# A twelve-layer decoder kernel: the first rounds of its state-space layer written out by hand, and that layer's end interleaved with the start of the 8-head attention layer

## The chip, the cores and the metric

The kernel runs on one core of one Trainium2 chip. The time is that of one launch on the device, in microseconds (us); of several runs the median is taken. The engines of the core, as the profile names them, are PE (TensorE, matrix products; PEld is its weight load), DVE (VectorE), ACT (ScalarE), POOL (GpSimd) and SP (SyncE, which here only issues DMAs). Each engine works through its own list of instructions in order and waits for the others through semaphores.

## The reference

The input x is 32 sequences of 128 tokens with 128 features, in float32. Twelve layers follow, each of the form x = x + f(layernorm(x)). Only the first two are touched by the change:

```python
x = x + _L0_attn_ref(_layernorm(x), ...)              # state-space layer
x = x + _L0_xattn_ref(_layernorm(x), ctx_1024, ...)   # 8-head attention
```

The state-space layer projects each token to a gate z, to 512 channels and to 32 step sizes dt. It runs a causal convolution of four taps over the channels and applies silu. The channels are then x (256), B (128) and C (128). The recurrence over tokens is computed in chunks: products C·B weighted by exponentials of running sums of dt·A, times dt·x, and a carried state. The result y gets a skip term, is gated and normalized, goes through an output projection and a layer norm and is added:

```python
y = Y + D_skip * x;  y = y * silu(z)
y = y * rsqrt(mean(y * y) + 1e-5) * norm_w
out = y @ out_proj_w.T
ln = (out - mean) * rsqrt(var + 1e-5) * ln_w + ln_b
return x + ln            # x here is the normalized input of the layer
```

The 8-head layer takes queries from x, and keys and values from both x and a context of the same shape (256 keys in all), with heads of 64:

```python
q1, k1, v1 = x1 @ Wq1, x1 @ Wk1, x1 @ Wv1;  k2, v2 = x2 @ Wk2, x2 @ Wv2
attn = softmax(q1 @ concat(k1, k2).T * 64**-0.5)
out = (attn @ concat(v1, v2)) @ Wo + bo
```

The tenth layer's feed-forward half multiplies by an int8 weight, `wq`, which the change also touches.

## The kernel before, in words

The 32 sequences are held as 8 groups (G) of 4 (J). A group is a tile `xg[i]` of 128 partitions (tokens) by 4 x 128. The layers run one after another over all groups. Within a layer the work is a list of rounds, one per sequence, numbered n = 4·i + j (group i, sequence j). A helper `go` (line 893) advances a generator by one step, so that a step of a later group can stand in a round of an earlier one. `follow(T, A, V)` (line 901) makes PE, ACT and DVE keep the order in which the program issues their instructions, until `follow()` (line 950). POOL and SP, and whatever is issued outside such a stretch, are placed by the framework's scheduler. Nearly every instruction is recorded under line 194, a helper, so that the profile is read by tile names.

**The state-space layer, `layer0` (line 662).** Its steps are these.

- `entry(g)` (742): mean and variance on DVE, a power on POOL (732), four ACT instructions that write the normalized `xn`, an addition on POOL, four PE transposes and an ACT copy to `xnT`.
- `decays(g)` (751): the step sizes and their exponentials (tiles `dts`, `dA`).
- `conv(g, c)` (689), for each of four channel blocks c: one PE product of 128x512 and an ACT copy to a `bmid` tile; an ACT scaling into a `gmid` tile; three DVE multiply-adds; an ACT tanh; a last DVE multiply-add. Each of these is a step.
- `gate(g, b)` (709): the same for z.
- `first(n)` (781), `second(n)` (810), `exponentials(n)` (821), `weighted(n, h)` (826), `third(n)` (831): the chunked products of one sequence, spread over three rounds. POOL builds their operands (lines 799, 804, 806).
- `joined(g)` (853): closes a group. DVE combines the sums (tile `bmid`), ACT squares them, PE does the output projection and the sums of squares (`ps<-w,bmid` and, with a single output column, `ps<-cs,bmid`), then come the norms on DVE, POOL and ACT and three POOL instructions that update `xg[g]`.

The loop at line 902 runs n from -9 to 33. Rounds -9 to -3 do only entry, decays and conv steps, one at a time, since `first(0)` comes in round -2. Rounds 32 and 33 only close the last group.

**The 8-head layer, `layer1` (954).** `prepare(i, 0)` loads a group of the context by DMA and normalizes x (BN statistics on DVE, then lines 394 to 397 on POOL). `prepare(i, 1)` transposes both. `project_in(n)` (967) makes queries and keys, `project_values(n)` (981) values, `scores(n, c2)` (989) half of the scores, with exponentials (1004) and scaling (1011). Ahead of its loop the layer does all of this for the first sequences in one straight run, and only then begins its rounds: transposes of the probabilities (1018), the weighted sum (1030), the output projection (1042), and the scores of the next sequence.

**Buffers.** Tiles come from pools with a fixed number of buffers under one name: PSUM `ps`, `two` and `acc` two each; `gbig` 3, `bbig` 4, `gmid` 10, `bmid` 5, `xn` and `xnT` 2 each. A tile waits until the buffer that it takes over is no longer read. During the state-space layer all three `gbig` and one `bbig` are held throughout (its `kept` and `more`), and the weights `w0` occupy one of the four `units` buffers.

**Loads.** SP issues, in this order: the constants `cs` (line 278), the eight groups of x (284), weight units 0 to 2 (304), the 16 KB of `wq` (1654), and the first context group (323). ACT issues `w0`, `ww` and two more weight loads. The cast of `wq` to bf16 stands in `layer9`, outside any kept order.

Of the kernel before, what the change touches and what calls it, by code (L numbers as in the profile page):

```python
# [25 lines left out]
G = 8  # L26
J = 4
# [177 lines left out]
def program(ctx, tc, cols, x, ctxt, mask, drop, dfirst, dsmall, dwide, drows, dunits, dexperts, dconst, drel, dwq, out):  # L205
# [23 lines left out]
    def gbig(shape=(128, 2048), dtype=F32):  # L229
        return big.tile(list(shape), dtype, tag="gbig", name="gbig", bufs=3)  # L230
# [7 lines left out]
    def bmid(shape=(128, 512)):  # L238
        return mid.tile(list(shape), F32, tag="bmid", name="bmid", bufs=5)
# [5 lines left out]
    def follow(*engines):  # L245

        for e in (V, A, T):
            e.keep(e in engines)
# [26 lines left out]


    cs = const.tile([128, cconst.n], F32, name="cs")
    SY.dma_start(out=cs, in_=dconst)
    K = {n: cconst.view(cs, n) for n in cconst.at}
    ident = K["ident"]  # L280
    xg = []
    for i in range(G):
        t = const.tile([128, J, D], F32, name=f"x{i}")
        SY.dma_start(out=t, in_=x[i * J : i * J + J].rearrange("b s d -> s b d"))
        xg.append(t)
        if i == 0:
            w0 = units.tile([128, cfirst.n], F32, tag="unit", name="w0")
            A.dma_start(out=w0, in_=dfirst)
            ww = const.tile([128, cwide.n], F32, name="ww")
            A.dma_start(out=ww, in_=dwide.to_broadcast([128, cwide.n]))  # L290
            wr = const.tile([1, crows.n], F32, name="wr")
            A.dma_start(out=wr, in_=drows)
# [24 lines left out]
    flip = const.tile([128, 128], BF16, name="flip")  # L317
    V.tensor_copy(flip, W0["flip"])
    ctxT = [const.tile([128, 512], F32, name=f"ctxT{i}") for i in range(G)]

    def load_ctx(i):
        t = gmid((128, J, D))
# [336 lines left out]

    def layer0():
        na = const.tile([128, 32], F32, name="na")
        A.activation(na, WW["m_A_log"], AF.Exp)
        V.tensor_scalar(na, na, -1.0, None, ALU.mult)
# [187 lines left out]
        def joined(g):  # L853

            ys, sq = [], []
            for b in range(2):
                y = bmid((128, J, 128))
                for ch in (1, 0):
                    at = slice(64 * ch, 64 * ch + 64)
                    V.scalar_tensor_tensor(y[:, :, at], convs[g, b][:, :, at], W0["D"][:, b : b + 1], sums[g][ch][:, b], ALU.mult, ALU.add)  # L860
                ys.append(y)
            for b, y in enumerate(ys):
                V.tensor_tensor(y[:, :, 64:128], y[:, :, 64:128], offs[g][:, b], ALU.add)
                V.tensor_tensor(y, y, zs.pop((g, b)), ALU.mult)
            yield
            for y in ys:
                q = bmid((128, J, 128))
                A.activation(q, y, AF.Square)
                sq.append(q)
            yield  # L870
            op, msp = ps((128, J, 128)), ps((128, J))
            for j in range(J):
                for b in range(2):
                    mm(op[:, j], ys[b][:, j], W0["out"][:, b * 128 : b * 128 + 128], b == 0, b == 1)
            for j in range(J):
                for b in range(2):
                    mm(msp[:, j : j + 1], sq[b][:, j], K["ones"][:, 0:1], b == 0, b == 1)
            ln = bmid((128, J, 128))
            A.copy(ln, op)
            yield  # L880

            rs, r2 = small(J), small(J)
            V.tensor_scalar(rs, msp, 1.0 / 256, 1e-5, ALU.mult, ALU.add)
            V.reciprocal(r2, rs)
            P.tensor_tensor(rs, rs, K["nhalf"], ALU.pow)
            for _ in normalize(ln, ln, rs, r2):
                yield
            P.tensor_tensor(ln, ln, bc(WW["m_ln_w"], 1, J), ALU.mult)
            P.tensor_tensor(xg[g], xg[g], bc(WW["m_ln_b"], 1, J), ALU.add)
            P.tensor_tensor(xg[g], xg[g], ln, ALU.add)  # L890
            yield

        def go(what, g, *more):

            if 0 <= g < G:
                key = what, g, *more
                if key not in late:
                    late[key] = what(g, *more)
                next(late[key], None)

        follow(T, A, V)
        for n in range(-9, G * J + 2):
            i, j = n // J, n % J

            g, c = (i + 1, j) if j < 2 else (i + 2, j)
            go(conv, g, c)
            if 0 <= n + 2 < G * J:
                first(n + 2)
            go(conv, g, c)
            if j == 0:  # L910
                go(joined, i - 1)
                go(gate, i, 0)
            elif j == 1:
                go(joined, i - 1)
            elif j == 2:
                go(decays, i + 2)
                go(decays, i + 2)
            elif j == 3:
                go(decays, i + 2)
                go(gate, i + 1, 1)  # L920
                go(entry, i + 3)
            if 0 <= n + 1 < G * J:
                second(n + 1)
            go(conv, g, c)
            if 0 <= n + 1 < G * J:
                exponentials(n + 1)
                weighted(n + 1, 0)
            if 0 <= n < G * J:
                third(n)
            if 0 <= n + 1 < G * J:  # L930
                weighted(n + 1, 1)
            go(conv, g, c)
            if j == 0:
                go(joined, i - 1)
                go(joined, i - 1)
            elif j == 1:
                go(joined, i - 1)
                go(joined, i - 1)
                go(joined, i - 1)
                go(entry, i + 2)  # L940
            elif j == 2:
                go(decays, i + 2)
                go(decays, i + 2)
                go(gate, i + 1, 1)
            elif j == 3:
                go(entry, i + 3)
                go(entry, i + 3)
                go(gate, i + 1, 0)
            go(conv, g, c)
        follow()  # L950

    def layer1(then):
        ua, ub = U[0], U[1]
        ctxs, normal, sources, keys, queries, values, probs, outs, heads = ({} for _ in range(9))

# [9 lines left out]
        def project_in(n):  # L967
            i, j = n // J, n % J
            at = slice(j * 128, (j + 1) * 128)
            if n % 2 == 0:  # L970
                keys[n // 2] = gbig((128, 2, 4, 256))
            q, k = gmid((128, 4, 128)), keys[n // 2][:, n % 2]
            for w, src, o, copy in ((0, sources[i], q, A.copy), (1, sources[i], k[:, :, 0:128], V.tensor_copy),
                                    (2, ctxT[i], k[:, :, 128:256], A.copy)):
                p = ps((128, 4, 128))
                for c in range(4):
                    mm(p[:, c], ua[:, w * 512 + c * 128 : w * 512 + c * 128 + 128], src[:, at])
                copy(o, p)
            queries[n] = q
# [70 lines left out]
                add_x(i, outs.pop(i))  # L1050

        last = G * J
        follow(T, A, V)
        prepare(0, 0)
        prepare(0, 1)
        project_in(0)
        for c2 in range(2):
            for step in scores(0, c2):
                step()
        prepare(1, 0)  # L1060
        project_in(1)
        project_values(0)
        for n in range(last + 1):
            i, j = n // J, n % J
            ahead = n + 1 < last
            if n < last:
                if ahead:
                    e0 = scores(n + 1, 0)
                transposes(n, 0)
                if ahead:  # L1070
                    e0[0]()
            if n > 0:
                project_out(n - 1)
            if n < last:
                transposes(n, 1)
                if ahead:
                    e0[1]()
                    e1 = scores(n + 1, 1)
                if j == 1 and i + 1 < G:
                    prepare(i + 1, 1)  # L1080
                if n + 2 < last:
                    project_in(n + 2)
                if ahead:
                    e1[0]()
                    project_values(n + 1)
                    e1[1]()
                weighted(n)
                if j == 0 and 0 < i and i + 1 < G:
                    prepare(i + 1, 0)
                if i == G - 1:  # L1090
                    next(then)
        follow()


    def layer2():
# [554 lines left out]


    def layer9():
        wq8 = const.tile([128, 32], I32, name="wq8")
        SY.dma_start(out=wq8, in_=dwq)
        V.tensor_copy(wq, wq8.bitcast(I8))
        p = ps()
        mm(p[:, 0:32], W["a3_Wk"], W["a3_kp"])
        kf = const.tile([128, 32], F32, name="kf")
# [158 lines left out]
        return first, second, third, lambda: project(i, st["yT"], W["x3_W"], WW["L3_xattn_bout"])  # L1817


    wq = const.tile([128, 128], BF16, name="wq")  # L1820

    def layer11(i):

        rnd = 1.5 * 2.0**23
# [38 lines left out]
        return first, second, third, last  # L1863

    load_units(0, 1, 2, 3, 4)
    layer0()
    load_units(5)
    lead2, run2 = layer2()
    layer1(lead2)
    load_units(6, 7)  # L1870
    lead3, run3 = attention16(layer3(), layer4())
    run2(lead3)
# [41 lines left out]
```

## Time and profile before

| | us |
|---|---|
| median of 3 runs | 3098.97 |
| lowest and highest run | 3094.29, 3100.82 |
| the profiled execution | 3108.52 |
| its span, first to last instruction | 3106.7 |

So 1.8 us of the profiled execution lie outside its span, and it took 9.5 us longer than the median. The mean granted TensorE clock over the span was 0.903.

In the span, PE was busy for 2576.8 us (83%), DVE for 2106.3 (68%), ACT for 1509.0 (49%) and POOL for 996.4 (32%). The state-space layer takes roughly the first 450 us of the span and the 8-head layer runs from there to about 870 us.

A line of the chain of waits gives start, duration and what the chain went through at that time. A line of the timeline gives start, duration, engine, line, operation, output <- input with the shape, the count and, in brackets, how long the engine had been idle and what released it. A line of the stage table gives a stretch of the span, its length, each engine's busy time in it with the number of instructions, the granted TensorE clock (1.00 is full speed), the mean share of the DMA engines and GB/s.

### The profile page before, as it was taken

The page shows a single profiled execution, that of the slowest core. Times are in us where ns is not written, and L with a number is a line of the kernel's source. Part 1 is how long each engine was busy: PE and PEld are TensorE (multiplying, and loading weights), DVE is VectorE, ACT ScalarE, POOL GpSimd, SP SyncE. Part 2 cuts the span into 40 slices and gives each one's busy share as a digit, 9 for nine tenths or more (in the row PEclk, how much of TensorE's full clock was granted, in tenths as well). Part 3 has the DMA queues.
Part 4 walks back from the last instruction along what each step waited for, and adds up shares of the span by engine and source line. Part 5 has one row for each costly group of instructions (what it writes and reads, how often), then busy time and mean ns, then how long its engine had stood idle before and what let it go on. Part 6 is the DMA issues. An engine that isn't in the chain of part 4 may idle for free.

```text
span 3106.7 us, 55574 instructions
## 1 busy us (share of the span) xinstructions
PE 2576.8 (83%) x22554; PEld 1651.8 (53%) x22554; DVE 2106.3 (68%) x4228; ACT 1509.0 (49%) x3411; POOL 996.4 (32%) x1034
## 2 busy tenths in 40 slices
PE   4887889999989988888887999978886869886554
PEld 2555556777744445556664444445553657543433
DVE  4776747888788756667877555458895328777883
ACT  3555534444422245556654445447772226555563
POOL 3343332322210122234542000034434355424444
PEclk8888879999989999999999999979997889997777
DMA  3000000000000000000000000000003243100000
GB/s 108 2 2 2 5 19 4 8 8 1 11 11 1 0 31 2 5 8 9 8 5 15 1 1 1 0 1 2 1 2 125 79 150 106 62 18 14 21 11 21
DMA packets 50146, 68.35 MB, mean 22 GB/s; under 512 B 3681, under 2 KB 41570, under 8 KB 49762
## 3 DMA queue, kind: packets, MB, share of 16 engines
q1 hardware_dynamic: 42608, 33.84, 3.5%
q0 software_dynamic: 6848, 27.81, 2.7%
q8 instruction: 178, 2.92, 0.4%
q10 hardware_dynamic: 434, 3.14, 0.3%
q14 instruction: 78, 0.64, 0.1%
HBM read 51.11 MB, written 13.68 MB: 21 GB/s over the span
## 4 chain that ended last, share of the span: by engine, by line
PE 51%; DVE 30%; ACT 7%; POOL 7%; issue 3%; DMA 1%; another core or an unknown queue 1%; SPq 0%; POOLq 0%; DVEq 0%; ACTq 0%
PE ps L194 22%; PE two L194 15%; PE acc L194 14%; DVE bbig L194 12%; DVE s L194 9%; DVE bmid L194 4%; DVE gmid L194 3%; ACT bbig L194 3%; POOL xn L397 3%; POOL gbig L477 2%; ACT bmid L194 2%; POOL s L395 1%; ACT gmid L194 1%; ACT gbig L194 1%; DVE x L194 1%
## 5 line engine op out<-in xcount | busy, mean ns | idle before, releaser
L194 PE MATMUL ps<-cs,bbig 128*128 128x128 f32 x2208 | 330.9, 290 | 77.8 <-ACT bbig L194 43.4
L194 ACT COPY bbig<-ps 128x512 f32<-128x512 f32 x416 | 226.9, 586 | 270.3 <-PE ps L194 270.0
L194 PEld LDWEIGHTS ps<-cs,bbig 128*128 128x128 f32 x2208 | 255.9, 147 | 183.7 <-ACT bbig L194 98.0
L194 DVE TENSOR_REDUCE s<-two 128x8 f32<-128x1024 f32 (+1 forms) x192 | 234.2, 1220 | 143.5 <-PE two L194 142.4
L194 PE MATMUL two<-xnT,u 128*128 128x512 f32 x512 | 264.5, 617 | 14.0 <-DVE bmid L194 7.8
L194 DVE TENSOR_TENSOR bbig<-bbig 128x256 f32<-128x256 f32 (+4 forms) x394 | 274.3, 749 | 2.0 <-ACT bbig L194 1.0
L194 PE MATMUL acc<-bmid,u 128*128 128x512 f32 x448 | 238.5, 619 | 29.6 <-DVE bmid L194 28.2
L194 PE MATMUL two<-gbig,gmid 32*128 32x512 f32 (+1 forms) x1280 | 205.9, 578 | 32.9 <-POOL gbig L477 32.0
L477 POOL TENSOR_SCALAR gbig<-bmid,cs 128x512 f32<-128x512 f32 x96 | 148.6, 1564 | 209.0 <-ACT bmid L194 209.0
L194 DVE TENSOR_TENSOR bmid<-bmid,ps 128x512 f32<-128x512 f32 x192 | 129.9, 684 | 109.1 <-ACT bmid L194 90.3
L194 ACT ACTIVATE bbig<-bbig 128x1024 f32<-128x1024 f32 (+1 forms) x160 | 141.8, 887 | 94.7 <-DVE bbig L194 94.2
L194 ACT ACTIVATE bbig<-two,s 128x256 f32<-128x256 f32 (+1 forms) x384 | 153.9, 439 | 26.9 <-DVE s L194 23.5
L194 ACT ACTIVATE bmid<-two 128x512 f32<-128x512 f32 x104 | 61.7, 596 | 196.3 <-PE two L194 186.4
L194 PEld LDWEIGHTS two<-xnT,u 128*128 128x128 f32 x512 | 92.6, 194 | 119.1 <-issue 55.2
L194 PEld LDWEIGHTS acc<-bmid,u 128*128 128x128 f32 x448 | 80.7, 195 | 130.2 <-DVE bmid L194 72.6
L194 DVE TENSOR_TENSOR bbig<-two,s 128x1024 f32<-128x1024 f32 (+1 forms) x128 | 139.7, 1092 | 8.6
L194 ACT ACTIVATE bmid<-two,ws 128x512 f32<-128x512 f32 x128 | 85.2, 686 | 117.7 <-PE two L194 115.8
L1014 POOL TENSOR_TENSOR bbig<-bbig,s 128x1024 f32<-128x1024 f32 x32 | 60.6, 1893 | 238.6 <-PE two L194 154.4
L194 ACT ACTIVATE bbig<-bbig,s 128x128 f32<-128x128 f32 x384 | 118.8, 388 | 24.2 <-DVE s L194 24.2
L194 PE MATMUL ps<-cs,xn 128*128 128x128 f32 x288 | 66.2, 318 | 72.8 <-ACT xn L194 31.4
L489 POOL MEMSET val<- 128x512 f32 x72 | 39.0, 543 | 260.8 <-PE acc L194 260.0
L194 PEld LDWEIGHTS two<-gbig,gmid 32*128 32x128 f32 (+1 forms) x1280 | 82.0, 191 | 73.9 <-POOL gbig L477 35.2
(291 smaller groups left out, 5976.9 us busy)
## 6 DMA issues: line engine op xcount, KB each, us to landing
u<-in_units SPq DMA_DIRECT2D x10, 768.0 KB
gmid<-in_ctx SPq DMA_DIRECT2D x16, 256.0 KB, 2.6
xs<-bbig SPq DMA_DIRECT2D x4, 903.0 KB, 6.0
xt<-xs SPq DMA_DIRECT2D x28, 129.0 KB, 3.0
x<-in_x SPq DMA_DIRECT2D x8, 256.0 KB, 10.6
gmid<-in_mask SPq DMA_DIRECT2D x8, 256.0 KB, 3.3
ys<-bbig SPq DMA_DIRECT2D x2, 1024.0 KB
gmid<-ys SPq DMA_DIRECT2D x8, 256.0 KB, 5.3
```

Of the source, the lines that this page charges most:

```text
L194: d = f(*args, **kwargs)
L395: P.tensor_tensor(rs, rs, K["nhalf"], ALU.pow)
L397: P.tensor_scalar(xn[:, j, :], xg[i][:, j, :], mv[:, j, 0:1], rs[:, j : j + 1], ALU.subtract, ALU.mult)
L477: P.tensor_scalar(o[:, n, :], k, K["n4"][:, n : n + 1], None, ALU.mult)
L489: P.memset(o, 0.0)
L1014: (V if c2 else P).tensor_tensor(pr[:, four, :], pr[:, four, :], bc(nm[:, four], 2, 256), ALU.mult)
```

## The change

Four things are done.

1. **Loads at the start.** The DMA of `xg[0]` is issued before that of the constants `cs`. The load of `wq` keeps its place on SP's queue, and its cast, which stood in `layer9`, is issued in round 3 of the 8-head layer, inside the kept order.
2. **First rounds of the state-space layer.** Rounds -9 to -3 of the loop are replaced by a list of 33 steps written out by hand. It contains the same steps: `entry(0)`, `entry(1)`, `decays(0)` and the four convolutions of group 0, but with the convolutions overlapping one another. The loop starts at -2.
3. **The start of the 8-head layer moves into the last rounds of the state-space layer.** `layer1` returns a generator `lead`. Its parts are issued at the ends of rounds 27 to 31 (load and normalize group 0; transposes; `project_in(0)`; `project_in(1)`; load and normalize group 1) and, after the loop, between the steps of `joined(7)`: the scores of sequence 0, then their exponentials, the values and the scaling. The keys of the first two sequences go to a `bbig` buffer, since the three `gbig` are still held.
4. **The closing of the last group moves into the first rounds of the 8-head layer.** `joined(7)` uses `gmid` instead of `bmid` tiles. Its last norm, three steps, is returned to `run1`, which advances it by one step at the end of rounds 0 and 1 and finishes it in round 2.

The diff, cut to its core:

```diff
     cs = const.tile([128, cconst.n], F32, name="cs")
-    SY.dma_start(out=cs, in_=dconst)
...
         if i == 0:
+            SY.dma_start(out=cs, in_=dconst)
...
-    def layer0():
+    def layer0(lead):
...
             ys, sq = [], []
+            tile_of = gmid if g == G - 1 else bmid
...
-            yield
+            if g < G - 1:
+                yield
...
-        for n in range(-9, G * J + 2):
+
+        go(entry, 0)
+        go(entry, 0)
+        go(entry, 0)
+        go(entry, 1)
+        go(entry, 0)
+        go(decays, 0)
+        go(conv, 0, 2)
+        go(entry, 1)
+        go(decays, 0)
+        go(conv, 0, 2)
+        go(conv, 0, 3)
+        go(conv, 0, 2)
+        go(conv, 0, 3)
+        go(entry, 1)
+        go(conv, 0, 2)
+        go(conv, 0, 3)
+        go(conv, 0, 0)
+        go(conv, 0, 2)
+        go(conv, 0, 0)
+        go(decays, 0)
+        go(conv, 0, 3)
+        go(conv, 0, 0)
+        go(entry, 1)
+        go(conv, 0, 3)
+        go(decays, 0)
+        go(conv, 0, 1)
+        go(conv, 0, 1)
+        go(conv, 0, 0)
+        go(conv, 0, 1)
+        go(decays, 0)
+        go(conv, 0, 0)
+        go(conv, 0, 1)
+        go(conv, 0, 1)
+        for n in range(-2, G * J):
...
             go(conv, g, c)
+            if n >= G * J - 5:
+                next(lead)
+        go(joined, G - 1)
+        next(lead)
+        go(joined, G - 1)
+        next(lead)
+        go(joined, G - 1)
         follow()
+        return late[joined, G - 1]
...
-                keys[n // 2] = gbig((128, 2, 4, 256))
+                keys[n // 2] = (gbig if n else bbig)((128, 2, 4, 256))
...
-        follow(T, A, V)
-        prepare(0, 0)
-        prepare(0, 1)
-        project_in(0)
-        for c2 in range(2):
-            for step in scores(0, c2):
-                step()
-        prepare(1, 0)
-        project_in(1)
-        project_values(0)
-        for n in range(last + 1):
+
+        def lead():
+            prepare(0, 0)
+            yield
+            prepare(0, 1)
+            yield
+            project_in(0)
+            yield
+            project_in(1)
+            yield
+            prepare(1, 0)
+            yield
+            steps = [step for c2 in range(2) for step in scores(0, c2)]
+            yield
+            steps[0]()
+            steps[2]()
+            project_values(0)
+            steps[1]()
+            steps[3]()
+            yield
+
+        def run(others, then):
+            follow(T, A, V)
+            for n in range(last + 1):
+                go_round(n, others, then)
+            follow()
...
                 weighted(n)
+                next(others, None)
+                if n == 2:
+                    for _ in others:
+                        pass
+                if n == 3:
+                    V.tensor_copy(wq, wq8.bitcast(I8))
...
-        wq8 = const.tile([128, 32], I32, name="wq8")
-        SY.dma_start(out=wq8, in_=dwq)
-        V.tensor_copy(wq, wq8.bitcast(I8))
...
     load_units(0, 1, 2, 3, 4)
-    layer0()
+    SY.dma_start(out=wq8, in_=dwq)
+    lead1, run1 = layer1()
+    rest0 = layer0(lead1)
     load_units(5)
     lead2, run2 = layer2()
-    layer1(lead2)
+    run1(rest0, lead2)
```

More of the change, by code (lines that the diff above doesn't have):

```diff
@@ L319, in program @@
     ctxT = [const.tile([128, 512], F32, name=f"ctxT{i}") for i in range(G)]
+    wq8 = const.tile([128, 32], I32, name="wq8")
+    wq = const.tile([128, 128], BF16, name="wq")
     def load_ctx(i):
@@ L855, in joined @@
             ys, sq = [], []
+            tile_of = gmid if g == G - 1 else bmid
             for b in range(2):
-                y = bmid((128, J, 128))
+                y = tile_of((128, J, 128))
                 for ch in (1, 0):
@@ L866, in joined @@
             for y in ys:
-                q = bmid((128, J, 128))
+                q = tile_of((128, J, 128))
                 A.activation(q, y, AF.Square)
@@ L877, in joined @@
                     mm(msp[:, j : j + 1], sq[b][:, j], K["ones"][:, 0:1], b == 0, b == 1)
-            ln = bmid((128, J, 128))
+            ln = tile_of((128, J, 128))
             A.copy(ln, op)
-            yield
+            if g < G - 1:
+                yield
             rs, r2 = small(J), small(J)
@@ L949, in layer0, with layer1 @@
             go(conv, g, c)
+            if n >= G * J - 5:
[5 more added lines that the diff above has]
+        go(joined, G - 1)
         follow()
-    def layer1(then):
+        return late[joined, G - 1]
+    def layer1():
         ua, ub = U[0], U[1]
@@ L1052, in layer1, with go_round @@
         last = G * J
-        follow(T, A, V)
-        prepare(0, 0)
-        prepare(0, 1)
-        project_in(0)
-        for c2 in range(2):
-            for step in scores(0, c2):
-                step()
-        prepare(1, 0)
-        project_in(1)
-        project_values(0)
-        for n in range(last + 1):
+        def lead():
[22 more added lines that the diff above has]
+            follow()
+        def go_round(n, others, then):
             i, j = n // J, n % J
@@ L1091, in layer1 @@
                     next(then)
-        follow()
+        return lead(), run
     def layer2():
@@ L1817, in layer10 @@
         return first, second, third, lambda: project(i, st["yT"], W["x3_W"], WW["L3_xattn_bout"])
-    wq = const.tile([128, 128], BF16, name="wq")
     def layer11(i):
```

## The prediction, made before the changed kernel was run

> **What bounds the kernel now.** First the page: no engine is full over the span, so the place has to be read stage by stage. I cut the span where the change cuts it, with the stage table:
>
> ```profile
> 0.00:66.00 66.00, 25.92 (x80) 13.88 (x81) 27.33 (x82) 21.55 (x42) 19.78 (x25) 0.84 0.37 127
> 66.00:411.00 345.00, 280.86 (x4893) 181.30 (x4892) 246.37 (x472) 182.18 (x339) 132.90 (x129) 0.85 0.01 3
> 411.00:438.60 27.60, 25.46 (x608) 18.29 (x584) 14.16 (x30) 9.72 (x16) 10.16 (x12) 0.75 0.01 3
> 438.60:481.10 42.50, 25.62 (x110) 19.91 (x110) 14.96 (x50) 10.75 (x29) 16.79 (x19) 0.61 0.10 31
> 492.50:870.00 377.50, 369.22 (x3132) 288.58 (x3128) 303.54 (x550) 176.38 (x588) 97.20 (x83) 0.99 0.03 8
> ```
>
> The columns are PE, PEld, DVE, ACT, POOL, granted clock, DMA. Two stretches are bounded by no engine: the first 66 us (no engine above 42%) and the 42.5 us from the end of `third(31)` at 438.6 to the first round of the 8-head layer at 481.1, where PE is busy 25.62 us at a clock of 0.61 and DVE 14.96. The rounds after it keep PE busy 98% at clock 0.99. All that the change moves lies in those two stretches and in 411 to 438.6, rounds 28 to 31.
>
> Then the chain of waits at the start:
>
> ```profile
> 18.17 8.43 DMA wq<-in_wq
> 26.60 0.02 issue
> 26.62 0.23 DVE wq L194
> 26.85 0.67 DVE gmid L194
> ```
>
> The scheduler put the cast of `wq` on DVE in front of the first convolution's multiply-adds. The timeline says DVE idled 6.35 us for it. After that the chain is one convolution after another, each DVE 2.3, ACT 0.6, DVE 0.7, with waits between, until round -2; the first copy of `first(0)` (ACT `cbl`) starts at 52.27.
>
> Then the chain across the seam, cut to its longest pieces:
>
> ```profile
> 443.00 6.58 PE ps L194 x30
> ...
> 454.72 3.14 POOL xn L397 x4
> ...
> 459.06 5.51 PE ps L194 x24
> ...
> 467.93 1.94 ACT bbig L194 x8
> ...
> 472.16 1.93 ACT bbig L194 x8
> ...
> 477.37 3.78 PE ps L194 x4
> ```
>
> It is a single file: `joined(7)`, then norm, transposes, projection, scores, exponentials, values, each waiting for the one before, with PE at half its clock.
>
> **Part A, the start.** x of group 0 now goes ahead of `cs`. Before, `cs` landed at about 7.5 and x at 10.67; in the other order `cs` lands at about 10.7 (the same bytes on the same queue), and POOL then still has its six copies from `cs` (1.47) ahead of the power, against BN statistics and aggregates (1.4) before. The power ends at about 13.3 either way (13.23 before). I take 0, bounds -1.5 (later) and +2 (earlier); the first ACT instruction waits for `ww` at 10.0 in both, so there is no more to win.
>
> The 33 hand-written steps: `xnT` of group 0 ends at 16.3 as before. I lay the steps on the engines with the rows' durations: `decays` products 1.8 to 18.1, product of channel block 2 to 20.0, copy 0.6, scaling 0.8, so DVE begins its multiply-adds at 21.6. From there DVE is the longest queue: four convolutions of 2.3 + 0.7 make 12.0, the `decays` operations 1.6 (0.22 + 0.29 + 0.23 + 0.22 + 0.45 plus the next add). That is 13.6, ending at 35.2. ACT has 4 x (0.6 + 0.8 + 0.6), `xn` of group 1 1.65 and small ones, about 11, beside it; PE 5 products and 12 small ones, beside it. The last transposes of `first(0)` then give the copy at 35.8 instead of 52.27: 16.5 earlier. The old schedule pays the 6.35 for `wq` and some 10 of waits inside single convolutions. I take 15, for about 1.5 of handoffs that a queue sum leaves out. Bounds 10 (every second handoff between ACT and DVE waits as before) and 17.5. The cast of `wq` becomes 0.23 us of DVE in round 3, where DVE is 80% busy and PE sets the pace: 0. Its DMA stays where it was on SP's queue.
>
> **Part B, the seam.** What leaves the single file between 438.6 and 481.1 goes to two places.
>
> Into rounds 27 to 31, on the engines' lists:
>
> - BN of group 0 on DVE (1.2) stands before `joined(6)`, where DVE is on the chain: +1.2.
> - Its POOL part (0.23 + 1.04 + 3.13, then 1.26 at line 965) falls into POOL's idle 5.83 us between 412.1 and 417.9. The builds of `first` queue behind it, but not before 420: 0. If POOL were later, PE would stand at the transposes, which are now ahead of `first(31)` on its list; that is worth up to 3.
> - Eight transposes after PE's `joined(6)` products: +2.2, since the clock there is 0.50.
> - `project_in(0)` behind `third(29)`: 3.15 warm (486.6 to 489.6 in the steady rounds), 5.5 cold (459.06). I take 4.3.
> - `project_in(1)` behind `third(30)`: 3.2, but PE idled about 3 us there, waiting for DVE's weights before `third(31)`; 2.5 of it fill that.
> - The context DMAs wait for `gmid` buffers on SP, which has nothing urgent behind them; the next unit load waits for `w0` anyhow.
>
> Sum: 1.2 + 2.2 + 4.3 + 3.2 - 2.5 = 8.4, I take 8; `third(31)` ends at 446.6.
>
> After it, DVE's list is BN of group 1 (1.2), the five steps of y (3.8), two reductions (1.24 each), two copies of values (0.69 each); with the last writes of `third(31)` (0.5), the first reduction is done at +6.8 and the exponentials (1.9) at +8.9. PE has put one product of `scores(1, 0)` before the output projection of `joined(7)`, and that waits for a `two` buffer until +8.9. Here PE idles from about +4 to +9, so the projection (3.3) and the sums of squares (3.4), both durations of 443 to 449.5, run cold, to +15.8; the rest of the scores 1.6. The transposes of sequence 0 start at +17.4, at 464.0. Before they started at 482.68. That is 18.7 earlier.
>
> From this I take off 2 for a clock still at half in round 0, and 1 for the rest of `joined(7)` in rounds 0 to 2 (ACT 1.65, DVE about 0.5, POOL 3.6; ACT is busy 47% in these rounds and POOL 26%, so only a handoff shows). B gives about 16. Bounds 9 (all cold, PE waiting for POOL at the transposes) and 25 (PE stays warm: 446.6 - 2.5 + 13 = 457, no deductions).
>
> Here a rule of the Trainium skill stands against the row. "TensorE: Matmul & The Clock Gate", Part 1, says that about 3.4 us of idle PE halves the clock and about 3.4 us of sustained work restores it. By the rule the return costs 3.4 us at half pace, 1.7 lost. But in the trace PE counts as busy 5.00 of 5 from 420 to 430 at a granted clock of 0.50, after the one-column products of `joined(6)`, so 14 us passed before it came back; that would cost 7. At 459, with dense 128-column products, it came back within 6 us, which costs 3. The new rounds are dense, so I use that row; part of the 3 lies in the cold projection already counted, hence the 2. The same rule forbids booking the whole 42.5 as idle time won: the change still leaves a gap of 5 us in front of `joined(7)`.
>
> **The sum.** 15 + 16 = 31 off the profiled execution: 3108.5 - 31 = 3077.5. The median of the runs stands 9.5 below it, and I carry that over: 3099 - 31 = **3068**.
>
> **The rivals.**
>
> - *Only the start pays (10%).* PE is the bound of rounds 28 to 31 already (25.46 of 27.60), so all of the lead's PE work adds there cold (2.2 + 5.5 + 5.5), and the clock stays at half for 14 us into the 8-head layer (7). Then B is near 5 and the time 3099 - 15 - 5 = 3079. The row at 420 to 430 speaks for it; the idle 3 us at 433 to 438 and the 42.5 us of single file against.
> - *More than the sum (17%).* PE stays warm across the seam, B 25 and A 17: 3057. Against it: the 5 us gap on PE while DVE works through y and the reductions.
> - *Slower (3%).* The keys of the first pair sit in `bbig` and `joined(7)` in `gmid`, so both rotations are shifted when the 8-head rounds begin. If each of the 32 rounds then waited once more for a buffer on PE, 1.0 us a round would eat the 31, and 1.3 would give 3109. Against it: the waits that the two builds attach to the instructions differ only in the first few rounds and are the same from then on.
> - *It does not do what it says (2%).* The scheduler could again put the `wq` cast or a load in front of something. In the build the cast does stand in round 3, and SP's list is as written.
>
> **How the numbers follow.** The likeliest case (68%) is 3068. The range takes the bounds of A and B, not both at their worst at once: gains of 17 to 43, so 3056 to 3082. Measurement of this kernel can tell about 0.2% (6 us) from no change. Faster by more than that 0.95, within it 0.02, slower 0.03.
>
> **What would show it right or wrong.** The first `cbl` copy at 35 to 38 (A right), at 42 or later (A wrong). No DVE wait on `wq` at the start. Spacing of `third(28)` to the end of `third(31)` grown from 27 to about 35 us. First 128x1024 reduction of `two` about 7 us after `third(31)`, and the transposes of sequence 0 near 449 in the new profile (464 less the 15 of A). PE's clock below 0.7 for some 10 us around the seam. Rounds from 4 on unchanged at about 11.6 us each; if those have grown, the slower rival is at work and the prediction is wrong.

## The result and the profile after

| | us |
|---|---|
| changed kernel, median of 4 runs | 3059.25 (3057.08 to 3071.78) |
| before, 4 runs beside them | 3098.18 (3094.29 to 3100.82) |
| ratio | 0.9884 (95% interval 0.9855 to 0.9913) |
| profiled execution, its span | 3071.78, 3070.0 (clock 0.905) |

By medians 38.9 us are gone, by the two profiled executions 36.7. Predicted were 31 and 3068: the sign and the range hold, the gain is larger by 6 to 8.

The stage table of the changed kernel, cut at the places that answer to the cuts of before (columns PE, PEld, DVE, ACT, POOL, granted clock, DMA share, GB/s):

```profile
0.00:50.00 50.00, 25.82 (x80) 14.15 (x81) 28.36 (x81) 21.12 (x42) 19.39 (x25) 0.80 0.48 167
50.00:392.30 342.30, 278.64 (x4707) 182.31 (x4710) 242.20 (x462) 178.29 (x331) 129.55 (x126) 0.84 0.01 3
392.30:433.80 41.50, 39.67 (x835) 30.64 (x832) 21.63 (x49) 17.38 (x29) 19.98 (x22) 0.84 0.03 9
433.80:450.50 16.70, 11.41 (x60) 8.92 (x60) 11.72 (x31) 5.60 (x19) 8.82 (x10) 0.80 0.09 26
459.80:838.40 378.60, 369.00 (x3148) 288.33 (x3148) 306.58 (x556) 178.81 (x596) 99.90 (x85) 1.00 0.03 9
```

The work of the start fits into 50 us instead of 66, with DVE at 57% instead of 41%. The stretch after `third(31)` shrank from 42.5 to 16.7 us. The 8-head rounds are as they were: 378.6 and PE at 98%.

The chain of waits of the changed kernel at the start:

```profile
19.63 0.59 ACT bmid L194
20.22 0.21 ACT dts L194
20.43 0.71 ACT gmid L194
...
21.16 0.76 DVE gmid L194
...
24.93 3.30 DVE gmid L194 x2
```

No wait for `wq` stands in front of the first multiply-add any more, and from 21.16 on the convolutions follow one another on DVE. The timeline has the first copy of `first(0)`:

```profile
36.41 0.43 ACT L194 COPY cbl<-ps 128x320 f32<-128x320 f32 x1
```

The chain across the seam:

```profile
402.13 5.35 POOL xn L401 x4
...
434.47 1.06 DVE s L194 x8
435.54 1.89 DVE gmid L194 x5
...
439.38 1.15 DVE s L194
...
440.97 1.94 ACT bbig L194 x8
...
442.95 1.22 PE two L194 x2
444.17 5.72 PE ps L194 x32
```

The single file now begins with DVE's list (statistics of group 1, y, a reduction), goes through one set of exponentials, and ends with the closing products of `joined(7)`. PE's idle time in it stands in the timeline, in brackets:

```profile
442.95 1.22 PE L194 MATMUL two<-bbig,gmid 64*128 64x256 f32 x2 [5.29 <-ACT bbig L194]
444.10 3.78 PE L194 MATMUL ps<-w,gmid 128*128 128x128 f32 x16
447.67 2.20 PE L194 MATMUL ps<-cs,gmid 128*128 128x1 f32 x16
...
450.86 1.09 PE L194 MATMUL ps<-cs,bbig 128*128 128x128 f32 x8
```

The last line is the transposes of sequence 0, at 450.86 (482.68 before).

What the seam brings is measured from the first products of `third(28)` to the first transposes of sequence 0. In the trace before these are:

```profile
410.74 1.49 PE L194 MATMUL acc<-bbig,gbig 64*32 64x64 f32 x128
...
482.68 1.09 PE L194 MATMUL ps<-cs,bbig 128*128 128x128 f32 x8
```

In the changed kernel the first and the end of `third(31)` are:

```profile
399.05 1.76 PE L194 MATMUL acc<-bbig,gbig 64*32 64x64 f32 x128
...
433.16 0.66 PE L194 MATMUL ps<-cbl,cs 128*128 128x64 f32 x4
```

Where the time went is seen from the same instructions in both traces. After the start the changed kernel is 16 us ahead, at `third(28)` 11.7, at the end of `third(31)` 4.8, at the first transposes 31.8, and nearly constant, 31.3 to 31.7, through most of the 8-head rounds. In the layers that the change does not touch the lead wanders between 30 and 36 and ends at 37.

### The profile page after: what moved, and what is told of

The parts are those of the page before. It is cut to its first block, busy times and chain, and to the rows that moved or that the text cites. A ratio compares the mean times of both kernels' runs of the same rounds, so it can differ in the third digit from the quotient of the medians.

```text
span 3070.0 us, 55552 instructions
## 1 busy us (share of the span) xinstructions
PE 2569.2 (84%) x22536; PEld 1652.1 (54%) x22554; DVE 2106.3 (69%) x4228; ACT 1510.2 (49%) x3411; POOL 998.0 (33%) x1034
## 3 DMA queue, kind: packets, MB, share of 16 engines
q10 hardware_dynamic: 434, 3.14, 0.3%
## 4 chain that ended last, share of the span: by engine, by line
PE 52%; DVE 29%; POOL 8%; ACT 7%; issue 3%; another core or an unknown queue 1%; DMA 1%; POOLq 0%; DVEq 0%; SPq 0%; ACTq 0%
PE ps L194 22%; PE two L194 16%; PE acc L194 14%; DVE bbig L194 12%; DVE s L194 9%; DVE bmid L194 3%; POOL xn L401 3%; DVE gmid L194 3%; ACT bbig L194 3%; POOL gbig L481 2%; ACT bmid L194 1%; POOL s L399 1%; ACT gmid L194 1%; ACT gbig L194 1%
## 5 line engine op out<-in xcount | busy, mean ns | idle before, releaser
L194 ACT ACTIVATE bbig<-two,s 128x256 f32<-128x256 f32 (+1 forms) x384 | 154.3, 441 | 22.7 <-DVE s L194 19.2
L1064 POOL TENSOR_TENSOR bbig<-bbig,s 128x1024 f32<-128x1024 f32 x32 | 60.6, 1894 | 218.1 <-PE two L194 144.6
L493 POOL MEMSET val<- 128x512 f32 x72 | 39.1, 545 | 259.9 <-PE acc L194 259.2
L194 ACT COPY bbig<-bbig 128x256 f32<-128x256 f32 (+3 forms) x320 | 97.9, 376 | 47.0 <-DVE bbig L194 45.5
L194 PE MATMUL ps<-cs,xn 128*128 128x128 f32 x288 | 66.4, 317 | 65.2 <-ACT xn L194 31.8
```

What stands on the lines that cost most here:

```text
L194: d = f(*args, **kwargs)
L493: P.memset(o, 0.0)
L1064: (V if c2 else P).tensor_tensor(pr[:, four, :], pr[:, four, :], bc(nm[:, four], 2, 256), ALU.mult)
```

## The experiments

The theory was that two independent gains add (start about 16, seam about 20), and that whatever else moves is the granted clock. The rivals were: a better or worse buffer layout (from the lead's loss of 4 between `first(0)` and `third(28)`), and that the work hosted in rounds 28 to 31 is not hidden.

**One half alone.** The first kernel is the one before with the order of loads, the 33 steps and the `wq` cast in round 3; the second is the one before with only the seam changed (parts 3 and 4).

```diff
 e1: the kernel before, and
+        go(entry, 0)
...
+        for n in range(-2, G * J + 2):
...
+                if n == 3:
+                    V.tensor_copy(wq, wq8.bitcast(I8))
 e2: the kernel before, and
+        for n in range(-9, G * J):
...
+            if n >= G * J - 5:
+                next(lead)
```

> The start of the change alone (x before the constants, the 33 steps laid out by hand, the wq cast in round 3 of the 8-head layer); the seam as before. My theory: start and seam are independent terms, 15.9 us and 20 us. So the first cbl copy starts at 36.4 (52.3 before), the seam from third(31) to the first transposes takes the old 44 us, and the time is 3098 - 15 = 3083, within 4 for what the clock does in between. Rival, the layout gives some back: the 4.4 us that the changed kernel lost against before between the first cbl copy and round 28 come from the new layout itself, then they are lost here too in the same place, and the time is 3087 with an offset of -11.5 at 411.

> The seam of the change alone; rounds -9 to -3, the order of the loads and the early wq cast as before. My theory: the first cbl copy is at 52.3 and the wait for wq is there; from round 28 to the steady 8-head rounds the kernel wins 20 us; the time is 3098 - 20 = 3078, within 4. Rival: the seam's gain depends on the phase in which the clock windows fall after the shorter start, then it is off by more than 4 here, 3070 or 3086.

Start only: 3086.93, ratio 0.9959 (0.9944 to 0.9975), first `cbl` copy at 36.38. Seam only: 3080.01, ratio 0.994 (0.9917 to 0.9963), first `cbl` copy at 51.41, and from `third(28)` to the first transposes 51.87 us, as in the changed kernel (51.81; before 71.95). The gains are 4.1 and 6.0 in a thousand, together 10.1. The changed kernel itself, run beside them, gave 10.3. The parts add within their intervals, and "only the start pays" falls. The time of the start alone is the 3087 that the layout rival had named. But its trace spent 129.7 us at half clock between the first `cbl` copy and `third(28)`, against 109.2 before, and took 7.3 us longer there; what such time costs is worked out below.

**The cast of `wq` alone**, in the kernel before:

```diff
+                if n == 3:
+                    V.tensor_copy(wq, wq8.bitcast(I8))
...
-        V.tensor_copy(wq, wq8.bitcast(I8))
```

> Before, with only the wq cast moved to round 3 of the 8-head layer. My theory: DVE no longer waits until 26.6, its first multiply-adds start at 19.9, but the convolutions still run one at a time, so the first cbl copy moves by about the 6.4 us of that wait, to 46. Rival: the wait hid other waits of the single-file convolutions, and the copy moves by less than 3, to 49.5 or later.

The first `cbl` copy came at 45.21 instead of 52.27. So 7.1 of the 15.9 us are the wait for `wq`, and 8.8 the hand-written order (with the order of the two loads, which is tried by itself below). The timeline of this kernel shows what the order then wins:

```profile
26.79 2.30 DVE L194 SCALAR_TENSOR_TENSOR gmid<-bmid,w,gmid 128x508 f32<-128x508 f32 x3 [1.37 <-ACT gmid L194]
...
29.84 0.69 DVE L194 SCALAR_TENSOR_TENSOR gmid<-bmid,gmid 128x512 f32<-128x512 f32 x1 [0.68 <-ACT bmid L194]
32.69 3.18 DVE L194 SCALAR_TENSOR_TENSOR gmid<-bmid,w,gmid 128x508 f32<-128x508 f32 x3 [2.16 <-ACT gmid L194]
```

DVE still stands idle inside each convolution, for ACT's scaling and tanh. Its one time, 3099.47, says nothing: 29 runs of the kernel before on that chip lay between 3086.85 and 3113.48.

**The order of the two loads**, turned back in the changed kernel:

```diff
+    SY.dma_start(out=cs, in_=dconst)
...
-            SY.dma_start(out=cs, in_=dconst)
```

> The changed kernel with the constants loaded ahead of group 0 of x again, as before the change. The prediction put the order of the loads at 0 (bounds -1.5 to +2). The changed kernel's trace has the power end 0.5 us earlier than before (12.74 against 13.23). If the order is what gives that, the power ends at 13.2 here and the first cbl copy at 36.9 instead of 36.4; if the chain is bound elsewhere, 36.4.

Here `cs` lands at about 7.5 instead of 10.0, the power ends at 12.53 (12.74 in the changed kernel), and the first `cbl` copy is at 36.20, against 36.23 to 36.44 in three traces of the changed kernel. The order of the loads is worth nothing measurable there, in either direction; the one time, 3063.69, lies among those of the changed kernel.

**The changed kernel again, unaltered, on two chips.**

> The changed kernel once more, nothing edited. My theory: the 4.4 us lost between the first cbl copy and round 28 are TensorE clock windows that fall differently in each execution (118.7 us at half clock there in the changed kernel, 109.3 before), so in another execution the loss is another number, by 1 us or more, in step with the time at half clock. Rival, the layout gives it back: again 4.4 within 0.5. Time 3059 within 6, both.

> The changed kernel once more, unaltered, as the measure for the two others of this chip: 3059 to 3064, and in the trace the stretch between the first cbl copy and third(28) between 358 and 363 us, longer by about 0.38 us for every us more at half clock.

3063.63, ratio 0.9897 (0.9861 to 0.9934), and 3063.56, ratio 0.9897 (0.9872 to 0.9921). The stretch from the first `cbl` copy to `third(28)` took 358.0 and 359.8 us here, 362.6 in the first profile and 358.5 before. The clock records know only full and half; in this stretch half clock was granted for 105.8, 116.1, 118.5 and 109.2 us. A line through all 14 traces (358 to 375 us) gives 0.39 us for each us more at half clock, and all lie within 1.2 us of it, kernels with either layout. At the same half-clock time the layouts agree: e6, with the new one, had 109.2 us of it and took 358.5, as before. So the loss of 4 goes with the clock (9.3 us more of it make 3.6 by the line), and the layout rival falls.

**Closing steps of `joined(7)` ahead of the 8-head rounds** instead of within them:

```diff
+        for _ in late[joined, G - 1]:
+            pass
...
-        return late[joined, G - 1]
+        return iter(())
```

> The changed kernel with the last norm of joined(7) issued ahead of the 8-head rounds, not in rounds 0 to 2. My theory: the norm is a chain of two POOL powers (1 us each) with DVE steps between and 1.65 us of ACT; ahead of round 0's own work it makes DVE wait for POOL in front of the copies of the probabilities, so the weighted sum of sequence 0 starts 1 to 3 us later after the first transposes than 8.8 us. Rival: the scheduler mixes the two anyway and nothing is lost, under 0.5.

From the first transposes to the first weighted sum 9.88 us, against 8.82, 9.15 and 9.30 in the three traces of the changed kernel. The 9.30 (e14) has the same half-clock time there, 3.1 us against 3.2, so the like comparison gives 0.6, between the two expectations. Part 4 as a place for these steps is worth about 1 us or less. (One run, 3057.73, inside the spread of the changed kernel.)

**The lead after the rounds** instead of within rounds 27 to 31:

```diff
-            if n >= G * J - 5:
-                next(lead)
...
+        for _ in range(5):
+            next(lead)
```

> The changed kernel with the first five parts of the 8-head start (load, norm, transposes, two projections, second norm) issued after the last round, behind the y of joined(7), not at the ends of rounds 27 to 31. My theory: rounds 28 to 31 go back to about 28 us and the rest grows by the norm on POOL (4.4), transposes (1.3) and projections (6 to 8) in single file: third(28) to the first transposes 61, against 51. Rival (only the start pays): PE is the bound of rounds 28 to 31, so hosting costs there what it saves behind, 54 or less.

From `third(28)` to the first transposes 57.0 us, between the two expectations (61, and 54 or less). Its chain after the last round:

```profile
431.35 1.05 POOL s L399
...
432.50 3.15 POOL xn L401 x4
...
435.70 0.49 PE ps L194
436.21 0.59 ACT xnT L194
...
436.85 8.02 PE ps L194 x48
```

The norm on POOL and the projections stand in single file again. To the first weighted sum it is 68.3 us, against 60.6 in the profile that has the same half-clock time in rounds 28 to 31: hosting wins about 8 in these two executions. Behind the rounds this one had 13.7 us more at half clock, up to 6.8 of the 8. Whether that belongs to the longer single file or to this execution was not separated. Its one time, 3079.13, is 7.4 above the first profiled execution of the changed kernel. The four POOL instructions of the norm took 3.15 here and 5.34 in round 28 of the changed kernel.

**Is it the gap in front of `joined(7)`?** The gap was filled in two ways. In e7 the scores of sequence 0 and their exponentials were put two parts earlier, into round 30, and the values and the second norm into one part behind the sums y of `joined(7)`. In e8 and e12, which are the same kernel, the four value products of sequence 0 were issued four times each (the same values, computed again). e13 does both.

```diff
 e7: scores two parts earlier
             project_in(1)
-            yield
-            prepare(1, 0)
-            yield
             steps = [step for c2 in range(2) for step in scores(0, c2)]
-            yield
             steps[0]()
             steps[2]()
+            yield
+            yield
             project_values(0)
             steps[1]()
             steps[3]()
+            prepare(1, 0)
+            yield
             yield
 e8, e12: value products four times
+REPEAT = 4
...
-                mm(p, src[:, j * 128 : j * 128 + 128], ub[:, k * 512 : (k + 1) * 512])
+                for _ in range(REPEAT if n == 0 else 1):
+                    mm(p, src[:, j * 128 : j * 128 + 128], ub[:, k * 512 : (k + 1) * 512])
 e13: both
```

> The changed kernel with the scores of sequence 0 and their exponentials issued in round 30, ahead of the last third(31), and the values, the scaling and the second normalization behind the sums y of joined(7). My theory: in the changed kernel the 5.3 us in which PE idles after the values exist because DVE does y (4) and then two reductions, and ACT the exponentials, before a two buffer is free; with the scores done while DVE waits for third(31) anyway, the output projection of joined(7) starts about 5 us after third(31) instead of 10.3, at a cost of 2 us of PE ahead of third(31). From third(28) to the first transposes of sequence 0: 48 (51.8 and 48.9 in two executions of the changed kernel), 3 less than the changed kernel at the same clock. Rival: PE at half clock sets the pace of the projection and the sums of squares in any order, then within 1 of it.

> The changed kernel with each of the four products that make the values of sequence 0 issued four times into the same buffer: the result is the same, and PE has about 6 us more to do in the gap in front of the output projection of joined(7). The clock theory: PE no longer idles past a clock window, so the projection and the sums of squares take 3.9 us together instead of 6.0, and the first transposes come 1 to 2 us earlier. Rival: the clock fell for other reasons (the one-column products), then the extra products only fill the gap: 0, or up to 1 later.

> The changed kernel with the four value products of sequence 0 issued four times each, now with enough runs for an interval. Theory (without the PE gap the clock stays at full through the seam, and the freed 3 to 5 us are kept): 3 to 5 below the changed kernel's 3059 to 3064, so 3055 to 3060, and third(31) end to the first transposes 13 to 14 us. Rival (the single 3051 was a run with luckier clock windows in the later layers): 3059 to 3064, no difference.

> Scores one part earlier and the four value products issued four times each. If the two gains add at the weighted sum of sequence 0 (6 to 9 and 7 to 9 us before the changed kernel's), 3050 to 3055; if both win the same thing, the half-clock window in the seam, no better than either alone: 3055 to 3060, weighted(0) about 51 to 52 us after third(28) as in both.

The stretches of 3.4 us around the gap, in the changed kernel's first profile:

```profile
437.20:440.60 3.40, 0.46 (x2) 0.00 (x0) 3.30 (x6) 1.26 (x2) 3.40 (x4) 1.00 0.00 0
440.60:444.00 3.40, 1.05 (x2) 0.50 (x2) 2.83 (x6) 3.03 (x13) 1.94 (x3) 0.65 0.00 0
444.00:447.50 3.50, 3.50 (x17) 3.40 (x17) 1.73 (x2) 0.72 (x4) 1.44 (x1) 0.50 0.00 0
447.50:450.90 3.40, 3.40 (x25) 3.00 (x24) 0.95 (x6) 0.59 (x1) 0.53 (x1) 0.86 0.58 175
```

and in its second profile (e4):

```profile
430.40:433.80 3.40, 0.83 (x2) 0.50 (x2) 3.02 (x7) 2.81 (x13) 1.94 (x3) 0.76 0.00 0
433.80:437.20 3.40, 3.40 (x15) 3.08 (x15) 1.73 (x2) 0.95 (x5) 1.67 (x1) 0.50 0.00 0
437.20:440.60 3.40, 3.40 (x19) 3.40 (x17) 0.00 (x0) 0.59 (x1) 0.00 (x0) 0.50 0.43 116
440.60:444.00 3.40, 3.40 (x14) 2.55 (x14) 2.17 (x11) 0.00 (x0) 1.03 (x1) 0.50 0.54 193
```

PE is idle, then the clock halves, then PE is fully busy at half clock, which lasts 6.8 us in all in the one and 13.7 in the other. With the value products repeated (e12), the whole seam, from `third(31)` to the first transposes, is this line, and its products are those of the timeline below it:

```profile
442.74:456.49 13.75, 13.72 (x73) 8.69 (x73) 12.29 (x33) 5.60 (x19) 9.19 (x10) 1.00 0.11 30
```

```profile
444.60 3.70 PE L195 MATMUL ps<-u,xnT 128*128 128x512 f32 x8
448.13 3.60 PE L195 MATMUL ps<-u,ctxT 128*128 128x512 f32 x8
451.76 2.05 PE L195 MATMUL ps<-w,gmid 128*128 128x128 f32 x16
453.65 1.84 PE L195 MATMUL ps<-cs,gmid 128*128 128x1 f32 x16
```

There is no gap, the clock is 1.00, and the closing products take 2.05 + 1.84 instead of 3.78 + 2.20. Ten of the 14 traces side by side: the second to fourth column are us at half clock, in rounds 28 to 31, in the seam (from the end of `third(31)` to the first transposes) and from there to the first weighted sum; the last column is the time from `third(28)` to the first weighted sum.

| | rounds 28 to 31 | seam | behind it | us |
|---|---|---|---|---|
| before | 13.7 | 34.1 | 0 | 80.6 |
| e10, lead after the rounds | 13.7 | 13.7 | 6.8 | 68.3 |
| changed | 13.7 | 6.8 | 0 | 60.6 |
| e12, values x4 | 13.7 | 0 | 0 | 57.1 |
| e13, both | 6.8 | 0 | 3.4 | 56.1 |
| changed (e4) | 3.4 | 10.9 | 2.8 | 58.0 |
| changed (e14) | 0 | 10.6 | 3.1 | 57.0 |
| e9, close first | 0 | 10.5 | 3.2 | 57.6 |
| e7, scores ahead | 0 | 0 | 6.8 | 51.8 |
| e8, values x4 | 0 | 0 | 0 | 51.4 |

The four traces with the gap filled have no half clock in the seam, and every other trace has some. The value products are the clean test, since they add work on PE and move nothing. Against an execution of the changed kernel with the same clock in rounds 28 to 31 they win 3.5 us (60.64 to 57.12, 6.8 us at half clock taken away) and 5.7 (57.03 to 51.35, 13.7 taken away); 1 to 2 were expected, at the transposes. The scores ahead win 5.3 (57.03 to 51.76), but in another way. The transposes come 39.1 us after `third(28)`, where 48 were expected, and part of that is lost again behind them, where 6.8 us are at half clock. e13 missed its 51 to 52. With half of its 10.2 us at half clock taken off, an estimate, it comes to 51, no better than e8, so nothing shows that the two ways add.

In the whole time they can't be told from the changed kernel. Value products repeated: 3051.42 in a single run (e8), then 3056.44, ratio 0.9862 (0.9842 to 0.9882); both together: 3061.12, above both expectations, 0.9881 (0.9859 to 0.9903); the changed kernel on the same chip 0.9897 (0.9872 to 0.9921). Scores ahead: 3059.58, 0.9861 (0.984 to 0.9882). The intervals overlap, so a better version is suggested, not shown. The profiled execution of e12 lost in the middle what it won at the seam: there its half-clock time was 143.4 us, and by the 0.39 above that is 10 us more than in the first profile of the changed kernel.

## Why the prediction was right, and which size was off

- **The start.** Predicted 15, measured 15.9. The multiply-adds began at 21.16 (predicted 21.6; its own terms, 20.0 + 0.6 + 0.8, make 21.4), and the first `cbl` copy came at 36.41 (35.8 by the queue sum). The load order was worth 0, as predicted (e6).
- **The middle.** The prediction had no term for it. The profiled execution lost 4.2 there, mostly with its half clock; the other two executions took 0.5 less and 1.3 more than before.
- **Rounds 28 to 31.** Predicted 8 longer, and 35 us from `third(28)` to the end of `third(31)`; measured 6.9 and 34.8. The transposes did wait for POOL, as the upper bound allowed, but the last of them for only 0.35 us (the line below), although the norm took 5.34 instead of the 3.13 that I carried over from a place where DVE was idle. The 8 is not all work, though: with little or no half clock there (e4, e14) the same rounds took 29.7 and 28.6 us. That the 8 was met is in part the luck of this execution.

```profile
407.52 0.18 PEld L194 LDWEIGHTS ps<-cs,xn 128*128 128x128 f32 x1 [0.35 <-POOL xn L401]
```

- **The seam.** The wait that ends last was the predicted one. The first reduction was done 6.7 us after `third(31)` (predicted 6.8), PE was released by the exponentials at +9.1 (8.9), the closing products ended at +16.0 (15.8) and the transposes began at +17.0 (17.4; 19.2 in e4 and e14). PE's gap, predicted from +4 to +9, was 5.29 long.
- **The step that was off** is the term at the end of part B: "From this I take off 2 for a clock still at half in round 0, and 1 for the rest of `joined(7)`". Transposes to first weighted sum took 8.82 us against 8.67 before, so of the 3 only 0.15 was paid (0.5 and 0.6 in e4 and e14, where the half clock reached into this stretch). Rounds 28 to 31 cost 1.1 less than the 8, and the transposes came 0.4 earlier. From `third(28)` to the transposes 20.1 us were won (71.95 to 51.81), not 16. The mechanism was right; B was undersized by 4, and lay within its bounds of 9 to 25.
- **Rule and row for the clock.** The three profiles of the changed kernel show 6.8, 13.7 and 13.7 us at half clock after the gap, with PE busy nearly all the while. Counted at half pace, an estimate, that is 3.4 to 6.8 us lost. The row I used said 6 us, 3 lost. The Trainium skill, "TensorE: Matmul & The Clock Gate", Part 1, lets about 3.4 us of work restore the clock, which by the same estimate loses 1.7. Neither figure holds in every execution. In e4 and e14 the one-column products of `joined(7)`, 3.41 us of them, lie in the middle of the 13.7; in the first profile they come at its end. Whether that is the reason was not tried. The page's other half, that about 3.4 us of idle PE halves the clock, agrees: in all three the clock fell within the gap of 5.3 us. But it also falls without such idle time, as `joined(6)` shows below. The page also says that the window is free-running and that the slow stretch differs from run to run; the grid at the end of this text is what these traces show of it. The booking of the gap itself as not won was right: e8 and e12 got 3.5 and 5.7 more by filling it.
- **The sum.** 31 were predicted, and about 31.5 is the lead in the 8-head rounds, though as 15.9 - 4.2 + 20.1 and not as 15 + 16: two errors cancel, which is luck. The median came out 7 lower still. Over 46 runs of the kernel before, the time falls by 2.0 us for each 0.001 of mean granted clock (correlation -0.95), and the median clock of the changed kernel's 14 runs is 0.909 against 0.9025: 13 of the 38 us. The half-clock time taken out of the seam (34.1 to between 6.8 and 10.9) explains 0.004 of it, as half of 25 us over 3080; its 8 us are part of the 20.1 and not a gain beside it. What is left, 0.0025 or some 5 us, lies elsewhere. Whether the change causes it by shifting their phase is not settled: after the last weighted sum the half-clock time was 426.3 us before and 426.8, 409.6 and 392.7 in three profiles of the changed kernel.
- **The rivals.** "Only the start pays" fell with e2. "More than the sum" was right in that B came out above 16, but PE did not stay warm. "Slower" by shifted buffers fell: 32 weighted sums took 374.2 us before and 373.2 after. "It does not do what it says" fell: no wait for `wq`, and the cast in round 3.

## What to carry to other kernels

Where work stands in single file between two stages, the gain from spreading it is found by laying the moved steps on each engine's list, hosts included, and finding the wait that ends last afterwards; here that was DVE's list and one set of exponentials, not PE. A gap of 5 us that remains on PE costs more than its length, since the closing products after it run at half clock, so it can pay to fill it even with work that has no use (3.5 and 5.7 us in this stage, though not shown in the whole time). And one profile of such a kernel is one draw: check the half-clock time of a stretch before a difference of a few us in it is given a cause.

## What the runs showed of the hardware that was not expected

- The granted clock in the records is either 1.0 or 0.5, and its half-clock stretches are 3.4, 6.8, 10.2 or 13.7 us and longer, in steps of 3.41. Within each of the 14 traces all changes of the clock lie on one grid of 3.41 us. Against the first instruction of the program the grid lies differently in each trace, from 0.50 to 3.35 us.
- In rounds 28 to 31 the same instructions had 13.7, 3.4 and 0 us at half clock in three executions of the changed kernel, and took 34.8, 29.7 and 28.6 us. The traces show where the difference begins. Here are the one-column products of `joined(6)` (a line of the timeline) and the grid interval after the one that holds most of them (a line of the stage table), in the first profile:

```profile
404.26 1.92 PE L194 MATMUL ps<-cs,bmid 128*128 128x1 f32 x16 [0.43 <-DVE gmid L194]
407.46:410.88 3.42, 3.35 (x15) 2.55 (x16) 1.52 (x5) 1.76 (x5) 3.34 (x5) 0.50 0.00 0
```

  and in e14:

```profile
401.46 1.92 PE L194 MATMUL ps<-cs,bmid 128*128 128x1 f32 x16 [0.43 <-DVE gmid L194]
402.71:406.12 3.41, 3.05 (x25) 2.48 (x26) 2.61 (x12) 1.17 (x2) 3.33 (x5) 1.00 0.00 0
```

  In the first, all 16 lie in one interval (404.05 to 407.46, in which PE was busy for 2.90 us); in e14 the grid cuts them at 402.71. So it goes with `joined(6)` in all 14 traces. Where 1.60 us or more of them lie in one interval, the next is at half clock (10 traces); where the grid cuts them, with at most 1.40 in one interval, it is at full (e7, e8, e9, e14). Elsewhere in this layer 1.84 us of them in one interval left the clock at full, with PE busy for all 3.41. The half clock behind the transposes of e7 follows 1.84 us of such products too. This is read from the traces; no run moved these products.
- In the state-space layer 30 to 40% of the time is at half clock, and each us of it costs 0.39 us, not the 0.5 of half pace. That fits other engines setting part of the pace; it was not tried.
- POOL's four 128x128 scalings took 3.14 us where DVE was idle all the while (before, at 454.7), 5.34 where it was busy for 4.31 of them (round 28), and 3.73 where it was busy for 3.63 (at 437.1). So DVE's mere being busy doesn't settle it; which of its instructions do was not tried.
- The one-column products run by the clock as well: 16 of them took 1.84 us at full clock, 3.41 at half.
